# A chain of four modulated convolutions on one Trainium2 core: the prologue's instructions in another order

## The chip, the core and the metric

The kernel runs on one core of a Trainium2 chip. The core has a matrix engine (TensorE, PE in the profile, with its weight loads listed apart as PEld), VectorE (DVE), ScalarE (ACT) and GpSimd (POOL), each with an instruction list of its own that it works through in order, and DMA queues that are issued mainly by SyncE (SP). Engines wait for each other through semaphores. The metric is the device time of one execution in microseconds; the median of three runs before the change is 489.17 (488.39 to 489.69).

## The reference

The input `x` has 128 samples of 64 channels by 1024 positions. Each sample has a style vector of 128 numbers. Four layers are applied in a chain, and the input is added at the end. Each layer scales its 64x64x3 weight by input channel with a number from the style (modulation), and then by output channel so that the weight's sum of squares is one (demodulation):

```
s = style @ mw.T + mb
weight = SCALE * w * s[:, None, :, None]
demod = lax.rsqrt(jnp.sum(weight * weight, axis=(2, 3)) + EPS)
weight = weight * demod[:, :, None, None]
'same':       out = conv(x, weight) + b
'upsample':   out = blur(conv_transpose(x, weight, stride 2) + b, 2 * [1,3,3,1]/8, pad (1, 1))
'downsample': out = conv(blur(x, [1,3,3,1]/8, pad (2, 2)), weight, stride 2) + b
...
x + layers(x)          # same, upsample, same, downsample
```

Everything is linear in `x`, so away from the two ends the chain is one convolution with nine taps per sample, plus a constant per channel.

## The kernel before

The kernel builds that nine-tap weight for each sample and convolves once. Samples are worked on four at a time: a group `q` (32 of them) is two pairs, the two halves of the 128 partitions carrying different samples. The order of instructions is the order in which the program is written (a manual schedule): each engine's list is what the code issues to it, one after the other.

Building the weight of a group is a chain of three stages on TensorE, with a scaled copy out of PSUM behind each, done by ScalarE and, for group 0, by ScalarE and VectorE for one half each (`BOTH`):

- `scale3(q)`: `wd`, the last layer's weight scaled by the table `tA`, which needs layer 2's demodulation.
- `stage1(q)`: `psS`, the product of layer 2's and layer 3's weights, copied to `S` with the scale `tB`.
- `stage2(q)`: `psR`, `S` times the blurred upsampling taps `E`, copied to `R` with the scale `tC`, which needs the demodulation of layers 0 and 1.
- `stage3(q, part)`: `psW`, times layer 0's weight, copied to `Wf` with `t0`.

`E` doesn't depend on a sample: `blur_scale` makes four scaled copies `w1s` of layer 1's weight on ScalarE, `blur_matmul` adds them up on TensorE in `Y`, and `blur_copy` copies `Y` to `E`. In the profile of before its matmuls are L333, its copies L346 and L348.

The nine taps are applied as three interleaved planes of `x` with three taps each, by five products in place of nine. `combine_a` and `combine_b` form the weights `H` of products 1 to 3 on VectorE; `in_g01`, `in_g2`, `in1`, `in2`, `in3` and `in04` form their inputs `G` and `T` from the loaded `X`. `conv3`, `conv1`, `conv2`, `conv4` and `conv0` are the products, each of 12 matmuls with 340 columns (24 records, since a float32 matmul leaves two), L612. Between them `sum1` (the tile `y`, VectorE) and `sum2` read and combine the accumulators; `conv2` adds to the bank that `sum1` reads, so it waits for `sum1`.

The constants of the bias go through the layers in three small steps, `const_first(l)` on TensorE (L767) and `const_rest(l)` on VectorE (the tile `cc`, L783 and L784); `const_first(1)` needs what `const_rest(0)` writes, and stands in TensorE's list right behind `conv3(0)`.

The prologue works on the first 16 samples (`first`). `mod_matmul` (L193) makes the modulations `sc`; `mod_matmul(LATER, ...)` makes those of the other 112 samples, which a ScalarE copy takes to `raw` (L976). `var_matmul` (L220) or `first_var_matmul` (L233) make the sums of squares; `var_root` (L245, L246) and `newton` (L252 to L254) the demodulations `d` (layer 2) and `dm`. `q2_sum` adds the three taps' squared weights `wsq`. `zeros_to_y` clears the two banks of `Y` by matmuls with zeros. In the loop behind the prologue TensorE's list for one group holds its five products, `stage2` of the group after next and `stage3`, and `stage1` of the one behind that.

The prologue's order, up to the loop, is lines 946 to 1050 of the kernel. The functions that the change touches are these:

Of the kernel before, what the change touches and what calls it, by code (L numbers as in the profile page):

```python
# [63 lines left out]
def kernel(  # L64
# [121 lines left out]
    def by_layer(ps, bs):  # L186
        n = bs.stop - bs.start
        return ps[:, : NL * n].rearrange("c (l b) -> c l b", l=NL)

    def mod_matmul(bs, ps, ls=range(NL)):  # L190
        for l in ls:
            for cols in HALF:
                nc.tensor.matmul(  # L193
                    by_layer(ps, bs)[cols, l], mwT[:, l], styT[:, bs], start=True, stop=True
                )

    def mod_scale(bs, src, ls):
        m = mbs[:, ls, None].to_broadcast([P, ls.stop - ls.start, bs.stop - bs.start])
        nc_v.scalar_tensor_tensor(
            sc[:, ls, bs], by_layer(src, bs)[:, ls], SCALE, m, op0=ALU.mult, op1=ALU.add  # L200
        )
# [11 lines left out]
    def q2_sum(ls):  # L213
        nc_v.tensor_add(q2[T, ls], wsq[T, ls, 0, :], wsq[T, ls, 1, :])
        nc_v.tensor_add(q2[T, ls], q2[T, ls], wsq[T, ls, 2, :])

    def var_matmul(bs, ps, ls=range(NL), start=True):
        for l in ls:
            for cols in HALF:
                nc.tensor.matmul(  # L220
                    by_layer(ps, bs)[cols, l],
                    q2[T, l, :],
                    ssq[T, l, bs],
                    start=start,
                    stop=True,
                    skip_group_check=not start,
                )

    def first_var_matmul(bs, ps):

        for k in range(K):
            for cols in HALF:
                nc.tensor.matmul(  # L233
                    by_layer(ps, bs)[cols, 2],
                    wsq[T, 2, k, :],
                    ssq[T, 2, bs],
                    start=(k == 0),
                    stop=(k == K - 1),
                )

    def var_root(bs, src, ls=slice(0, NL), dst=None):

        src = by_layer(src, bs)[:, ls]
# [12 lines left out]
    def first_inverse(bs, src):  # L256

        var_root(bs, src, slice(2, 3), d2[:, None])
        newton(var[:, 2, bs], d2, n2)
# [52 lines left out]
    def blur_scale(ks):  # L312
        for i in ks:
            nc_a.activation(w1s[:, i], w1r, AF.Copy, scale=BLUR2[i])

    def blur_matmul(ps, ks):


        n = len(BLUR2)
        plan = [[], []]  # L320
        for b in range(n):
            for r, (lo, hi) in enumerate(((0, 5), (5, NT))):
                i, j = max(lo, b), min(hi, b + K)
                if i < j:
                    plan[r].append((b, i, j, lo))
        plan[1].reverse()
        for k in ks:
            for r, rows in enumerate(HALF):
                if k >= len(plan[r]):
                    continue  # L330
                b, i, j, lo = plan[r][k]
                for cols in HALF:
                    nc.tensor.matmul(  # L333
                        ps[r][cols, C * (i - lo) : C * (j - lo)],
                        idn[rows],
                        w1s[rows, min(b, n - 1 - b), i - b : j - b],
                        start=False,
                        stop=(k == len(plan[r]) - 1),
                        skip_group_check=True,
                    )  # L340

    def blur_copy(ps, engs):
        for r, (i, j) in enumerate(((0, 5), (5, NT))):
            dst, src = E[:, i:j].rearrange("c e i -> c (e i)"), ps[r][:, : (j - i) * C]
            if engs[r] is nc_a:
                nc_a.copy(dst, src)  # L346
            else:
                engs[r].tensor_copy(dst, src)  # L348
# [24 lines left out]
    def scale3(q, engs=(nc_a, nc_a)):  # L373
        wd = []
        src = w3 if q < DIRECT else w3x
        n = src.shape[1]
        for j in range(2):
            t = wd_pool.tile([P, 5, C], F32, tag="wd", name=f"wd{q}_{j}")
            scaled_copy(engs[j], t[:, :n], src, tA[:, q, j : j + 1])
            wd.append(t)  # L380
        chain[q] = wd
# [22 lines left out]
    def stage1(q, pool=None, engs=(nc_a, nc_a), between=None):  # L404

        wd = chain[q]
        ps = unit(pool or ps_w, f"psS{q}")
        for k, (at, at1) in enumerate(((0, 3), (3, 1), (1, 4))):
            tap_matmul(ps, wd, at, 2, woi[2][:, k, :], EVEN, first=k == 0)
            tap_matmul(ps, wd, at1, 1, woi[2][:, k, :], slice(1, 2), last=k == K - 1)  # L410
        if between:
            between()
        st, _ = s_tiles(q)
        for r in range(2):
            scaled_copy(engs[r], flat(st[r][:, 1:]), ps[r][:, : 5 * C], tB[:, q, r : r + 1])
        chain[q] = st
        return ps
# [24 lines left out]
        nc_g.tensor_add(t[:, :, 2], t[:, :, 2], t[:, :, 0])  # L442
        chain[q] = st

    def stage2(q, pool=None, engs=(nc_a, nc_a), among=(), between=None):
        st = chain[q]
        ps = unit(pool or ps_w, f"psR{q}")
        for n, e in enumerate((-2, -1, 0, 1, 2, 3, 4, 5, 6)):
            if n in among:
                among[n]()  # L450
            if e % 2 == 0:
                a, lo, m = slice(1, 4), e // 2 + 1, 3
            else:
                a, lo, m = slice(4, 6), (e + 3) // 2, 2
            for r, rows in enumerate(HALF):
                for c, cols in enumerate(HALF):
                    src = st[c if r == 0 else 1 - c]
                    nc.tensor.matmul(  # L458
                        ps[r][cols, lo * C : (lo + m) * C],
                        E[rows, e + 2, :],  # L460
                        src[rows, a, :],
                        start=(n == 0),
                        stop=(n == 8),
                        skip_group_check=True,
                    )
        if between:
            between()
        rt = []
        for r in range(2):
            t = r_pool.tile([P, 7, C], F32, tag="R", name=f"R{q}_{r}")  # L470
            scaled_copy(
                engs[r], t.rearrange("c t o -> c (t o)"), ps[r][:, : 7 * C], tC[:, q, r : r + 1]
            )
            rt.append(t)
        chain[q] = rt
        return ps
# [247 lines left out]
    def scaled_weights():  # L724
        for t, f in zip(w0s[1:], (1.0 / 3.0, -2.0)):
            nc_g.tensor_scalar_mul(t, woi[0], f)
        nc_g.tensor_scalar_mul(idn3, idn, 1.0 / 3.0)
# [232 lines left out]
    nc_v.tensor_scalar_mul(mbs, mb, SCALE)  # L960
    mod_matmul(first, pm[0][0], (2, 3))
    nc_a.activation(wsq[T, 2], wio[2][T], AF.Square)
    blur_scale(range(4))
    mod_matmul(first, pm[1][0], (0, 1))
    mod_scale(first, pm[0][0], slice(2, 4))
    mod_square(first, L2)
    first_var_matmul(first, pm[0][1])
    mod_scale(first, pm[1][0], L01)
    mod_square(first, L01)
    mod_square(first, L3)  # L970
    table_B(first)
    table_0(first)
    mod_matmul(LATER, pm[1][1])
    first_inverse(first, pm[0][1])
    nc_a.activation(wsq[T, 3], wio[3][T], AF.Square)
    nc_a.copy(raw[0][:, 0, :n_later], pm[1][1][:, :n_later])  # L976
    blur_matmul(psB, range(2))
    table_A(first, d2)
    scale3(0, BOTH)
    for l in range(2):  # L980
        nc_a.activation(wsq[T, l], wio[l][T], AF.Square)
    q2_sum(L3)
    scaled_weights()
    weight_sums(0)
    stage1(0, None, BOTH, lambda: blur_matmul(psB, range(2, 5)))
    blur_copy(psB, BOTH)
    q2_sum(L01)
    q2_sum(L2)
    scale3(1)
    scale3(2)  # L990

    def rest_of_var():
        var_matmul(first, pm[0][1], (0, 1, 3))

    def rest_of_scales():
        var_root(first, pm[0][1])
        var_newton(first)
        table_C(first, nc_v)

    stage2(0, None, BOTH, {4: rest_of_var}, rest_of_scales)  # L1000
    for of in (vector_c0, table_3, vector_a1, vector_Da, vector_b1, vector_c2):
        of(first)
    weight_sums(1, 2)
    stage1(1, ps_conv)
    in_g01(0, PAIR[0])
    in_g01(0, PAIR[1])
    stage3(0, 0, None, BOTH)
    in3(0)
# [1 line left out]
    const_first(0, first)  # L1010
    stage1(2)
    combine_a(0)
    in_g2(0)
    load(NX)
    split_weights()
    in1(0, nc_v)
    combine_b(0)
    const_rest(0, first, const_of(0, first))
    in2(0, nc_v)
    stage2(1, ps_conv)  # L1020
    conv3(0)
# [276 lines left out]
```

## Time and profile before

| what | us |
|---|---|
| median of three runs | 489.17 |
| lowest and highest run | 488.39, 489.69 |
| the profiled execution | 490.47 |
| its span, first to last instruction | 488.7 |
| TensorE busy in the span | 478.6 (98%) |
| VectorE busy | 383.4 (78%) |
| ScalarE busy | 289.6 (59%) |
| GpSimd busy | 143.2 (29%) |

The profiled execution is longer than the three timed runs, so a sum of its durations is compared with its own time first. A row of the view in order of time gives the start, the duration, the engine, the line, the operation with the tile that it writes and those that it reads, the shapes, the number of records merged, and in brackets how long the engine idled before it and what ended the idle time. A matmul's end is modelled, and successive ones overlap; where the text speaks of a pace, it goes from start to start.

### The profile page before, as it was taken

To read this page: it belongs to the slowest core of one execution; us is meant where nothing else is said; L and a number is where in the kernel's file an instruction comes from. 1 tells how busy PE (TensorE), PEld (TensorE's weight loads), DVE (VectorE), ACT (ScalarE), POOL (GpSimd) and SP (SyncE) were. 2 spreads that over 40 slices of the span, in tenths; PEclk is the share of its full clock that TensorE was granted. 3 is DMA by queue.
4 is the path that set the end of the run, shared out by engine and by line. 5 is a ranking of instruction groups with operands and counts; after the bars stand their busy time and mean duration, and the time that the engine had idled before them with its cause. 6 is when DMAs were issued, how large, how long until landed. Compare 5 with 4: busy or idle time off the path is not lost.

```text
span 488.7 us, 22181 instructions
## 1 busy us (share of the span) xinstructions
PE 478.6 (98%) x10048; PEld 383.5 (78%) x10048; DVE 383.4 (78%) x631; ACT 289.6 (59%) x578; POOL 143.2 (29%) x173
## 2 busy tenths in 40 slices
PE   8989999999999999999999999999999999999995
PEld 6967878777899877778888887878887877888863
DVE  3888887887888868976868988758988776988783
ACT  4546666567566657556566656656656666566542
POOL 2629125441335323113322123322123231212300
PEclk9989999999999999999999999999999999999999
DMA  7032544434334442344442344442344543245225
GB/s 247 19 130 71 202 165 175 175 125 141 116 147 175 175 172 81 116 164 170 175 148 78 128 172 175 175 147 67 141 172 175 175 174 117 95 159 175 90 87 173
DMA packets 20303, 70.42 MB, mean 144 GB/s; under 512 B 2288, under 2 KB 3824, under 8 KB 20208
## 3 DMA queue, kind: packets, MB, share of 16 engines
q1 hardware_dynamic: 19840, 68.53, 39.6%
q8 instruction: 79, 1.29, 1.0%
q10 hardware_dynamic: 368, 0.46, 0.3%
q14 instruction: 16, 0.13, 0.1%
HBM read 35.36 MB, written 33.62 MB: 141 GB/s over the span
## 4 chain that ended last, share of the span: by engine, by line
PE 95%; DVE 2%; DMA 1%; POOL 1%; issue 0%; ACT 0%; DVEq 0%
PE psA L612 45%; PE psR L458 16%; PE psW L499 15%; PE Y L612 11%; PE psS L386 5%; PE psE L843 2%; DMA par<-in_params 1%; DVE H L520 0%; PE Y L333 0%; PE psM L193 0%; POOL td L281 0%; DVE G L520 0%; DVE T L585 0%; DVE Wf L359 0%; DVE T L570 0%
## 5 line engine op out<-in xcount | busy, mean ns | idle before, releaser
L612 PE MATMUL psA<-T,H 64*64 64x340 f32 x2304 | 197.1, 449 | 0.2 <-DVE y L520 0.2
L612 PEld LDWEIGHTS psA<-T,H 64*64 64x64 f32 x2304 | 104.6, 134 | 44.0 <-issue 12.0
L442 POOL TENSOR_TENSOR S<-S 128x128 f32<-128x128 f32 x29 | 13.7, 471 | 290.5 <-ACT S L357 290.5
L458 PE MATMUL psR<-S,E 64*64 64x192 f32 (+1 forms) x2304 | 87.5, 299 | 0.5 <-ACT E L346 0.5
L458 PEld LDWEIGHTS psR<-S,E 64*64 64x64 f32 x2304 | 82.3, 133 | 5.7 <-ACT E L346 0.7
L357 ACT ACTIVATE R<-psR,tC 128x448 f32<-128x448 f32 x63 | 36.5, 630 | 68.8 <-PE psR L458 67.3
L612 PE MATMUL psA<-T,Wf 64*64 64x340 f32 x768 | 76.5, 447 | 0.0
L520 DVE SCALAR_TENSOR_TENSOR G<-X 128x1376 f32<-128x1376 f32 (+2 forms) x66 | 76.3, 1196 | 0.0
L357 ACT ACTIVATE Wf<-psW,t 128x384 f32<-128x384 f32 (+1 forms) x126 | 56.3, 497 | 14.6 <-PE psW L499 14.6
L499 PE MATMUL psW<-R,w0s 64*64 64x128 f32 (+1 forms) x1536 | 64.2, 289 | 0.0
L612 PE MATMUL Y<-T,Wf 64*64 64x340 f32 x768 | 62.2, 446 | 0.1
L499 PEld LDWEIGHTS psW<-R,w0s 64*64 64x64 f32 x1536 | 54.1, 133 | 5.9 <-ACT Wf L357 0.8
L520 DVE SCALAR_TENSOR_TENSOR Y<-m,psA 128x680 f32<-128x680 f32 (+1 forms) x33 | 28.0, 849 | 36.0 <-PE psA L612 35.5
L599 DVE TENSOR_TENSOR T<-G 128x1368 f32<-128x1368 f32 (+1 forms) x33 | 50.8, 1541 | 0.1
L681 ACT ACTIVATE o<-Y,tb,td 128x340 f32<-128x340 f32 x64 | 37.1, 630 | 22.3 <-ACT R L357 16.8
L520 DVE SCALAR_TENSOR_TENSOR y<-psA,m 128x680 f32<-128x680 f32 (+1 forms) x33 | 27.8, 844 | 28.7 <-PE psA L612 28.0
L585 POOL TENSOR_TENSOR T<-G 128x684 f32<-128x684 f32 x30 | 49.8, 1660 | 0.1
L590 POOL TENSOR_TENSOR T<-G 128x684 f32<-128x684 f32 x30 | 49.5, 1650 | 0.0
L386 PEld LDWEIGHTS psS<-wd,w2n 64*64 64x64 f32 x1160 | 41.3, 133 | 8.2
L612 PEld LDWEIGHTS Y<-T,Wf 64*64 64x64 f32 x768 | 36.1, 133 | 12.7 <-issue 0.6
L681 ACT ACTIVATE o<-psA,tb,td 128x340 f32<-128x340 f32 x63 | 36.6, 633 | 14.8 <-PE psA L612 14.8
L520 DVE SCALAR_TENSOR_TENSOR H<-Wf 128x384 f32<-128x384 f32 x64 | 40.5, 634 | 0.0
(148 smaller groups left out, 533.1 us busy)
## 6 DMA issues: line engine op xcount, KB each, us to landing
X<-in_x SPq DMA_DIRECT2D x64, 516.0 KB, 4.5
out<-o SPq DMA_DIRECT2D x60, 510.0 KB, 5.3
out<-o SPq DMA_DIRECT2D x6, 170.0 KB, 4.1
out<-o SPq DMA_DIRECT2D x2, 340.0 KB, 3.1
Xe<-in_x_ends SPq DMA_DIRECT2D x1, 512.0 KB, 6.4
par<-in_params SPq DMA_DIRECT2D x2, 192.0 KB, 3.6
out<-o ACTq DMA_DIRECT2D x2, 170.0 KB, 4.1
par_s<-in_params_s SPq DMA_DIRECT2D x1, 196.0 KB, 3.3
```

The lines of the kernel that those rows point to most:

```text
L357: nc_a.activation(dst, src, AF.Copy, scale=f)
L386: nc.tensor.matmul(ps[r][cols, at * C : (at + n) * C], weight[rows], wd[c if r == 0 else 1 - c][rows, taps], start=first, stop=last, skip_ ...
L442: nc_g.tensor_add(t[:, :, 2], t[:, :, 2], t[:, :, 0])
L458: nc.tensor.matmul(ps[r][cols, lo * C : (lo + m) * C], E[rows, e + 2, :], src[rows, a, :], start=(n == 0), stop=(n == 8), skip_group_check ...
L499: nc.tensor.matmul(ps[r][cols, at : at + m * C], w0s[kind][rows, k, :], rt[c][rows, first : first + K * (m - 1) + 1 : K, :], start=(n == 1 ...
L520: nc_v.scalar_tensor_tensor(out, x, f, y, op0=ALU.mult, op1=op)
L585: eng.tensor_add(t[:, :, 0, :NJ], plane(g, 2), plane(g, 1))
L590: eng.tensor_sub(t[:, :, 1, :NJ], plane(g, 2), plane(g, 1))
L599: nc_v.tensor_sub(t[:, pairs, :, :NJ], both(a, PL), both(b, 1))
L612: nc.tensor.matmul(ps[s][cols, :NB], w, Ts[q, tag][rows, c, i, g : g + NB], start=(g == 0 and m == 3), stop=(g == K - 1), skip_group_check ...
L681: nc_a.activation(dst, src, AF.Identity, bias=add, scale=d3)
L843: nc.tensor.matmul(ps[r][cols, : HB * n].rearrange("c (b j) -> c b j", j=n), weight(i, r, c)[rows], moving(i, r, c)[rows], start=(i == 0), ...
```

## The change

Only the prologue is written in another order; the loop and its functions stay. The matmuls of all blurred taps stand in one piece ahead of `stage1(0)`, and both halves of `E` are copied by ScalarE. Layer 2's sum of squares is first added up on VectorE (`q2_sum(L2)`) and then takes two matmuls; `first_var_matmul` goes. Four matmuls with zeros (128 columns) are added ahead of it. The modulations of the later samples are split into two pieces: layers 0 and 1 between `stage1(0)`'s matmuls and its copies, behind the variance of layers 0, 1 and 3, which stood inside `stage2(0)`; layers 2 and 3 behind `stage2(0)`, and their ScalarE copy there too. `in_g01(0, PAIR[0])`, the first half of the first `G`, moves from behind `stage1(1)` to right behind `stage1(0)`. GpSimd makes `a1` and `b1s` ahead of `t3`, and `const_rest(0)` moves from behind `combine_b(0)` to behind `combine_a(0)`.

```diff
-    def first_var_matmul(bs, ps):
-
-        for k in range(K):
-            for cols in HALF:
-                nc.tensor.matmul(
-                    by_layer(ps, bs)[cols, 2],
-                    wsq[T, 2, k, :],
-                    ssq[T, 2, bs],
...
-    def stage2(q, pool=None, engs=(nc_a, nc_a), among=(), between=None):
+    def stage2(q, pool=None, engs=(nc_a, nc_a), between=None):
...
     nc_a.activation(wsq[T, 2], wio[2][T], AF.Square)
-    blur_scale(range(4))
+    blur_scale(range(2))
     mod_matmul(first, pm[1][0], (0, 1))
+    zeros_to_y(2, 128, False)
     mod_scale(first, pm[0][0], slice(2, 4))
     mod_square(first, L2)
-    first_var_matmul(first, pm[0][1])
+    q2_sum(L2)
+    var_matmul(first, pm[0][1], (2,))
...
-    mod_matmul(LATER, pm[1][1])
     first_inverse(first, pm[0][1])
+    blur_scale(range(2, 4))
     nc_a.activation(wsq[T, 3], wio[3][T], AF.Square)
-    nc_a.copy(raw[0][:, 0, :n_later], pm[1][1][:, :n_later])
-    blur_matmul(psB, range(2))
+    blur_matmul(psB, range(5))
     table_A(first, d2)
     scale3(0, BOTH)
     for l in range(2):
         nc_a.activation(wsq[T, l], wio[l][T], AF.Square)
+    blur_copy(psB, (nc_a, nc_a))
     q2_sum(L3)
+    q2_sum(L01)
     scaled_weights()
     weight_sums(0)
-    stage1(0, None, BOTH, lambda: blur_matmul(psB, range(2, 5)))
-    blur_copy(psB, BOTH)
-    q2_sum(L01)
-    q2_sum(L2)
+
+    def rest_of_var():
+        var_matmul(first, pm[0][1], (0, 1, 3))
+        mod_matmul(LATER, pm[1][1], (0, 1))
+
+    stage1(0, None, BOTH, rest_of_var)
+    in_g01(0, PAIR[0])
     scale3(1)
     scale3(2)
-
-    def rest_of_var():
-        var_matmul(first, pm[0][1], (0, 1, 3))
...
-    stage2(0, None, BOTH, {4: rest_of_var}, rest_of_scales)
-    for of in (vector_c0, table_3, vector_a1, vector_Da, vector_b1, vector_c2):
+    stage2(0, None, BOTH, rest_of_scales)
+    mod_matmul(LATER, pm[1][1], (2, 3))
+    nc_a.copy(raw[0][:, 0, :n_later], pm[1][1][:, :n_later])
+    for of in (vector_c0, vector_a1, vector_b1, table_3, vector_Da, vector_c2):
         of(first)
     weight_sums(1, 2)
     stage1(1, ps_conv)
-    in_g01(0, PAIR[0])
     in_g01(0, PAIR[1])
...
     combine_a(0)
+    const_rest(0, first, const_of(0, first))
     in_g2(0)
     load(NX)
     split_weights()
     in1(0, nc_v)
     combine_b(0)
-    const_rest(0, first, const_of(0, first))
     in2(0, nc_v)
```

Line numbers of the changed kernel are 12 to 14 lower. On TensorE, from the modulations of the first samples (`psM_171`) to the first matmul of `stage1(0)` (`psS_0`), before:

```order
L193 MATMUL psM_171<-par_s 64x16 x4
L233 MATMUL psM_170<-ssq,wsq 64x16 x6
L193 MATMUL psM_171<-par_s 64x112 x8
L333 MATMUL Y<-w1s,par 64x192 x8
L386 MATMUL psS_0_248<-wd_0_235,par 64x128
```

and after:

```order
L193 MATMUL psM_171<-par_s 64x16 x4
L169 MATMUL Y<-Z 64x128 x4
L220 MATMUL psM_170<-ssq,q_129 64x16 x2
L321 MATMUL Y<-w1s,par 64x192 x10
L321 MATMUL Y<-w1s,par 64x128 x4
L321 MATMUL Y<-w1s,par 64x64 x4
L374 MATMUL psS_0_255<-wd_0_238,par 64x128
```

The eight matmuls of the later samples (112 columns) have left this stretch, and the ten blur matmuls that stood behind `stage1(0)` have come into it.

On ScalarE, from layer 2's demodulation (`d`) to the last `wd` of the prologue, before:

```order
L245 ACTIVATE d_131<-psM_170,eps 128x16
L975 ACTIVATE wsq<-par 64x192
L976 COPY raw_143<-psM_171 128x448
L357 ACTIVATE wd_0_235<-par,tA 128x192
L981 ACTIVATE wsq<-par 64x192 x2
L357 ACTIVATE S_284<-psS_0_248,tB 128x320
L346 COPY E<-Y 128x320
L357 ACTIVATE wd_0_293<-par,tA 128x192
```

and after:

```order
L233 ACTIVATE d_131<-psM_170,eps 128x16
L302 ACTIVATE w1s<-par 128x192 x2
L963 ACTIVATE wsq<-par 64x192
L345 ACTIVATE wd_0_238<-par,tA 128x192
L968 ACTIVATE wsq<-par 64x192 x2
L334 COPY E<-Y 128x320
L334 COPY E<-Y 128x256
L345 ACTIVATE S_291<-psS_0_255,tB 128x320
```

The copy to `raw` no longer stands between `wsq` and `wd`, and `E` is copied ahead of `S`, both halves here.

On VectorE, from the third `H` (which `conv3(0)` needs) on, before:

```order
L520 SCALAR_TENSOR_TENSOR H_403<-H_403,Wf_402 128x384
L520 SCALAR_TENSOR_TENSOR G_397<-X_105 128x2x342
L585 TENSOR_TENSOR T_0_489<-G_397 128x2x342
L520 SCALAR_TENSOR_TENSOR H_403<-Wf_402 128x384
L520 SCALAR_TENSOR_TENSOR H_403<-Wf_402,H_403 128x384
L520 SCALAR_TENSOR_TENSOR H_403<-H_403,Wf_402 128x384
L783 TENSOR_TENSOR cc_152<-Y,a_145 128x16
L784 SCALAR_TENSOR_TENSOR cc_152<-b1s,cc_152 128x16
```

and after:

```order
L506 SCALAR_TENSOR_TENSOR H_403<-H_403,Wf_402 128x384
L769 TENSOR_TENSOR cc_152<-Y,a_145 128x16
L770 SCALAR_TENSOR_TENSOR cc_152<-b1s,cc_152 128x16
L506 SCALAR_TENSOR_TENSOR G_294<-X_105 128x2x342
L571 TENSOR_TENSOR T_0_491<-G_294 128x2x342
L506 SCALAR_TENSOR_TENSOR H_403<-Wf_402 128x384
L506 SCALAR_TENSOR_TENSOR H_403<-Wf_402,H_403 128x384
L506 SCALAR_TENSOR_TENSOR H_403<-H_403,Wf_402 128x384
```

The two `cc` rows have moved ahead of five others; nothing else moved among these.

More of the change, by code (lines that the diff above doesn't have):

```diff
@@ L226, in var_matmul @@
                     skip_group_check=not start,
-                )
-    def first_var_matmul(bs, ps):
-        for k in range(K):
-            for cols in HALF:
-                nc.tensor.matmul(
-                    by_layer(ps, bs)[cols, 2],
-                    wsq[T, 2, k, :],
-                    ssq[T, 2, bs],
-                    start=(k == 0),
-                    stop=(k == K - 1),
                 )
@@ L448, in stage2 @@
         for n, e in enumerate((-2, -1, 0, 1, 2, 3, 4, 5, 6)):
-            if n in among:
-                among[n]()
             if e % 2 == 0:
```

## The prediction

> **What bounds the kernel now.** I read the page first, then the busy times in windows of 3.41 us, then TensorE, ScalarE and VectorE in order of time up to 35 us, since nothing behind that is edited.
>
> ```profile
> span 488.7 us, 22181 instructions
> PE 478.6 (98%) x10048; PEld 383.5 (78%) x10048; DVE 383.4 (78%) x631; ACT 289.6 (59%) x578; POOL 143.2 (29%) x173
> PEclk9989999999999999999999999999999999999999
> ```
>
> TensorE is busy 98% of the span and the loop behind the prologue leaves it no gap worth the name, so a microsecond counts if it brings forward the moment from which TensorE runs unbroken, and if it runs at full clock from there. The third tenth of the clock row is below 9: the clock dropped once, inside the prologue.
>
> ```profile
> 3.64:7.05 3.41, 2.75 (x38) 2.64 (x40) 1.49 (x9) 2.00 (x7) 1.04 (x5) 1.00 0.91 231
> 7.05:10.46 3.41, 3.41 (x62) 2.81 (x62) 1.64 (x7) 1.39 (x4) 2.29 (x5) 1.00 0.98 351
> ...
> 24.12:27.53 3.41, 1.53 (x47) 1.27 (x46) 3.24 (x8) 0.72 (x1) 0.00 (x0) 1.00 0.85 306
> 27.53:30.94 3.41, 3.41 (x38) 2.80 (x34) 2.97 (x6) 2.15 (x6) 0.00 (x0) 0.50 0.01 2
> 30.94:34.36 3.42, 3.23 (x60) 1.86 (x56) 2.58 (x5) 1.89 (x7) 1.20 (x3) 1.00 0.02 5
> ```
>
> The first numbers are the window and TensorE's busy time, the third from the end the granted clock. In 24.12:27.53 TensorE worked 1.53 us and idled 1.88; in the window right behind it, and in that one alone, the clock was 0.50. The first 10.5 us say 1.00, but the weight loads contradict it:
>
> ```profile
> L386 PEld LDWEIGHTS psS<-wd,par 64*64 64x64 f32 x36 | 1.6, 220 | 0.2
> ...
> L333 PEld LDWEIGHTS Y<-w1s,par 64*64 64x64 f32 x20 | 0.7, 134 | 0.0
> ```
>
> The first row is from 9 to 10.4 us, the second from 10.5 to 11.6: the same 64x64 load falls from 220 to 134 ns. So TensorE starts slow and goes to full speed at 10.46. A window with 2.75 us of work (3.64:7.05) did not lift the clock, a full one (7.05:10.46) did.
>
> **The prologue on TensorE.**
>
> ```profile
> 5.34 0.83 PE L233 MATMUL psM<-ssq,wsq 64*64 64x16 f32 x12 [0.17 <-ACT w1s L314]
> 6.09 1.76 PE L193 MATMUL psM<-par_s 128*64 128x112 f32 x16
> 7.79 1.56 PE L333 MATMUL Y<-w1s,par 64*64 64x192 f32 x16
> 9.12 1.82 PE L386 MATMUL psS<-wd,par 64*64 64x128 f32 x48
> 10.77 0.82 PE L333 MATMUL Y<-w1s,par 64*64 64x192 f32 x20
> 12.12 1.32 PE L458 MATMUL psR<-S,E 64*64 64x192 f32 x32 [0.53 <-ACT E L346]
> ...
> 15.02 1.22 PE L386 MATMUL psS<-wd,par 64*64 64x128 f32 x48
> 16.28 1.04 PE L499 MATMUL psW<-R,par 64*64 64x192 f32 x22
> ...
> 20.03 2.66 PE L458 MATMUL psR<-S,E 64*64 64x192 f32 x69
> ...
> 26.29 0.23 PE L767 MATMUL Y<-cc,wsum 64*64 64x16 f32 x2 [1.88 <-DVE cc L784]
> ...
> 28.23 3.33 PE L612 MATMUL psA<-T,H 64*64 64x340 f32 x24
> ...
> 31.44 0.99 PE L499 MATMUL psW<-R,w0s 64*64 64x128 f32 x22
> 32.61 1.95 PE L612 MATMUL psA<-T,H 64*64 64x340 f32 x24 [0.18 <-DVE y L520]
> ```
>
> Columns: start, duration, operation and, in brackets, the idle time before it and its releaser. The two gaps of size are at 12.12 (R waits for E) and 26.29. The last row is where TensorE's unbroken run begins; it waits for `y` on VectorE:
>
> ```profile
> 7.34 0.53 DVE L284 TENSOR_TENSOR tA<-sc,d 64x8 f32<-64x8 f32 x2
> ...
> 8.62 0.22 DVE L215 TENSOR_TENSOR q<-q,wsq 64x64 f32<-64x64 f32 x1
> ...
> 15.17 0.34 DVE L284 TENSOR_TENSOR tC<-dm 64x8 f32<-64x8 f32 x2
> 15.61 0.68 DVE L359 TENSOR_SCALAR R<-psR,tC 128x448 f32<-128x448 f32 x1
> 16.21 1.65 DVE L520 SCALAR_TENSOR_TENSOR G<-X 128x688 f32<-128x688 f32 x2
> 18.30 0.62 DVE L359 TENSOR_SCALAR Wf<-psW,t 128x384 f32<-128x384 f32 x1 [0.44 <-POOL b1s L737]
> ...
> 25.70 0.17 DVE L783 TENSOR_TENSOR cc<-Y,a 128x16 f32<-128x16 f32 x1
> ...
> 29.12 0.87 DVE L570 TENSOR_TENSOR T<-X 128x684 f32<-128x684 f32 x1 [0.34 <-issue]
> ...
> 31.69 0.87 DVE L520 SCALAR_TENSOR_TENSOR y<-psA,m 128x680 f32<-128x680 f32 x1
> ```
>
> From 18.30 to 32.57 VectorE has one listed pause, 0.34 us. Its list there is the same before and after, but for the order, so `y` moves by what the first Wf row moves, and no more than about 0.34 beyond that.
>
> **The change, part by part.** ScalarE's rows and the landing of the first X transfer:
>
> ```profile
> 7.90 0.53 ACT L976 COPY raw<-psM 128x448 f32<-128x448 f32 x1 [1.18 <-PE psM L193]
> 8.33 0.46 ACT L357 ACTIVATE wd<-par,tA 128x192 f32<-128x192 f32 x1
> 8.69 0.60 ACT L981 ACTIVATE wsq<-par 64x192 f32<-64x192 f32 x2
> 11.04 0.53 ACT L357 ACTIVATE S<-psS,tB 128x320 f32<-128x320 f32 x1 [1.76 <-PE psS L386]
> 11.64 0.43 ACT L346 COPY E<-Y 128x320 f32<-128x320 f32 x1
> 11.97 1.49 ACT L357 ACTIVATE wd<-par,tA 128x192 f32<-128x192 f32 x4
> 13.78 0.31 ACT L245 ACTIVATE dm<-psM,eps 128x64 f32<-128x64 f32 x1 [0.33 <-PE psM L220]
> ...
> X<-in_x SPq DMA_DIRECT2D x1, 516.0 KB, 6.2
> ```
>
> *Layer 2's variance.* Six matmuls (0.83) become two behind two VectorE adds (0.22 each and the step between). Four matmuls off at about 0.06 each against 0.5 of adds, part of it in TensorE's 0.17 pause: I take zero, bounds -0.1 and +0.3. Half of the w1s scalings move behind `d` on ScalarE, which idles there before the raw copy. The four added zero matmuls run while VectorE adds: zero. The adds push the second modulation, and with it GpSimd's tables tB and t0, back by half a microsecond; they are first read by the copies of S after 10 us, so that is hidden.
>
> *wd.* The raw copy leaves ScalarE's path: tA ends at 7.87, so wd starts there and not at 8.33.
>
> *Blur and S on TensorE.* The later samples' matmuls (1.70, from 6.09 to 7.79) leave. The blur starts near 6.1. Its first 16 records take 9.12 - 7.79 = 1.33; the other 20 took 0.6 start to start at full clock, and at the slow clock about 0.6 x 220 / 134 = 1.0, an estimate. So S starts at about 8.5 instead of 9.12, takes 10.77 - 9.12 = 1.65, and its copies start near 10.4 instead of 11.04.
>
> *E.* ScalarE is through with wsq at about 8.9, and two E copies of 0.43 end at 9.8, ahead of S: the 0.53 gap goes. S is copied by 10.95. Under it TensorE does six variance matmuls (0.3) and half of the later samples' (0.85 slow, 0.43 at full clock), until 10.9 to 11.4. R starts at 11.1, not 12.12: -1.0, bounds -0.6 and -1.2.
>
> *R, tC, S(1), W.* ScalarE's four wd (1.49) and dm (0.31) end at 12.8; VectorE in between does the first G (half of 1.65; X was issued at 4.3 and lands near 10.5, so it just makes it). From dm's end to tC's end it was 15.51 - 14.09 = 1.42, so tC is ready at 14.2 and R copied by 14.9 (16.29 before). TensorE: R about 2.4 (2.66 with its drain), the other half of the later samples 0.43, S(1) 16.28 - 15.02 = 1.26: W starts at 15.2. TensorE and not the copies decides, with 0.3 to spare. W: 15.2 against 16.28, -1.05. The raw copy then stands behind R on ScalarE (0.53), done by 15.5, before S(1) can be copied.
>
> *VectorE to `y`.* Wf at 17.25, `y` done at 31.5, and the convolution of 32.61 starts at 31.5: -1.1; with the 0.34 pause gone too, -1.45.
>
> *The constants' inputs.* cc (two rows, some 0.4 us) now stands ahead of G2; the same work, so `y` doesn't move. POOL's a1 and b1s, which it reads, go ahead of t3, which waits some 0.4 us longer and is first read at H's time, five microseconds later. No DMA changes its place in a queue; the next X load waits for G2 as before. TensorE no longer waits at 26.29: its third-product convolution ends at 24.41 - 1.05 = 23.36, W(1,0) takes 28.23 - 26.29 = 1.94, the next convolution 1.95 at full clock: done at 27.2. But then it has only the 0.99 us of 31.44 until `y` at 31.5. The idle time isn't gone; 1.88 in front becomes 3.3 behind, directly ahead of the unbroken run.
>
> *The clock.* In the windows of the row above, 27.53:30.94 then holds some 2.4 us of idleness (all but the 0.99 of work), more than the 1.88 that brought the clock to 0.50. So 30.94:34.36 runs at half clock, and there TensorE is the bound. The convolution of 24 takes 1.95 at full clock and 3.33 at half, so each slow microsecond loses 1 - 1.95 / 3.33 = 0.41, a window 1.4. Before, this price fell on the convolution of 28.23, whose end VectorE was hardly waiting for. If only half of the window lies behind 31.5, it is 0.7. If the clock stays low for a second window, as it did after 2.75 of 3.41 us of work at the start, it is 6.8 x 0.41 less what lies ahead of 31.5, some 2.4.
>
> The Trainium skill ("TensorE: Matmul & The Clock Gate", "What's actually happening" and "Why this matters for your kernels") lets the clock fall after an idle window of about 3.4 us, and warns of gaps over about 3 us. By that neither the 1.88 us nor the new gap would cost anything, and the sum would be -1.1. The trace disagrees at 1.88 us, so the sum goes by the trace. The same page calls the window free-running, so its place may differ from run to run; no run here shows that yet.
>
> **Sum.** -1.1 + 1.4 = +0.3. The profiled execution took 490.47 (span 488.7 and 1.8 around it), 1.3 above the median of 489.17 and above all three runs; on it 490.8, on the median 489.5.
>
> **Rivals.** *The clock stays full*, because the 1 us of work in the middle is enough or because the gap would have to be longer: -1.1, 488.1; with the pause gone 487.7. For it: only one drop is in the trace. Against: that drop came after less idleness. (The Trainium skill's limit of the page above would make it so.)
>
> *Two slow windows, slower than before:* -1.1 + 2.4, 490.5 to 490.8. For it: 2.75 of 3.41 us of work didn't lift the clock at the start. It decides from the point at which the slow window begins more than 3.41 - 2.75 = 0.7 us before `y` is done; in the windows of the rows above it would begin at 30.94, just short of that. Against: those 2.75 us were smaller matmuls than a convolution's.
>
> *The prologue gains little:* the later samples' matmuls in the gaps, 2 x 0.85 if TensorE is still slow there, and an X that lands late hold R and W; the gain shrinks from 1.1 to 0.4 (W waits 0.7 to 0.8 more), and with the slow window it is 490.2.
>
> **Chances.** One slow window 0.50 (489.0 to 490.2), clock full 0.20, two windows 0.20, little gain 0.10. 0.3% is 1.5 us, about what can be told from no change here; most of these cases lie within it. Faster by that, below 487.7: half of the second case and a little for gains not seen, 0.14. Slower, above 490.6: half of the third and the fourth, and a fifth of the first, whose prices add up to more if W is late as well, 0.26. Same 0.60. The range goes from 487.7 to 491.0.
>
> **What would show it.** R's first matmul near 11.1, W's near 15.2, the first Wf on VectorE near 17.25, `y` near 30.6; no wait before the cc matmul, a gap of over 2 us right before the convolution that follows `y`, and a clock of 0.5 for 3.4 us over it. The forecast is wrong if that convolution takes 1.95, if Wf comes later than 17.8, or if VectorE is not busy through from Wf to `y`.

## The result, and the profile after

The changed kernel takes 488.23 us (median of 22 runs, 486.93 to 489.87), the kernel before, run beside it on the same chip, 488.94 (22 runs, 487.94 to 489.69): a ratio of 0.9986 [0.9978, 0.9994], 0.7 us faster. The forecast was 489.5, 0.3 us slower. The number lies in the forecast's range; the direction was wrong.

The page of the changed kernel (profiled execution: 488.43 us):

```profile
span 486.6 us, 22180 instructions
PE 478.0 (98%) x10048; PEld 366.9 (75%) x10048; DVE 381.0 (78%) x630; ACT 289.9 (60%) x579; POOL 140.8 (29%) x173
```

Its TensorE rows in order of time:

```profile
7.89 2.13 PE L374 MATMUL psS<-wd,par 64*64 64x128 f32 x46
...
11.04 2.73 PE L444 MATMUL psR<-S,E 64*64 64x192 f32 x72
...
15.29 0.94 PE L485 MATMUL psW<-R,par 64*64 64x192 f32 x24
...
27.13 0.23 PE L753 MATMUL Y<-cc,wsum 64*64 64x16 f32 x2 [0.61 <-DVE cc L770]
...
30.18 2.99 PE L598 MATMUL psA<-T,H 64*64 64x340 f32 x24 [1.96 <-DVE y L506]
32.93 3.39 PE L444 MATMUL psR<-S,E 64*64 64x192 f32 x72
...
53.98 1.90 PE L598 MATMUL psA<-T,H 64*64 64x340 f32 x24
```

R starts at 11.04 without a wait and W at 15.29, both as forecast. The unbroken run begins at 30.18, behind a gap of 1.96 us that VectorE's `y` ends. Its first convolution takes 2.99 us. The windows of 3.41 us there (first numbers: the window and TensorE's work; third from the end: the granted clock):

```profile
24.12:27.53 3.41, 2.79 (x64) 1.63 (x57) 3.31 (x6) 2.16 (x6) 0.00 (x0) 1.00 0.55 222
27.53:30.94 3.41, 1.45 (x34) 0.84 (x29) 3.38 (x7) 2.68 (x8) 0.37 (x1) 1.00 0.03 7
30.94:34.36 3.42, 3.42 (x44) 2.09 (x40) 1.46 (x3) 0.06 (x1) 3.26 (x4) 0.50 0.58 181
```

The half clock has moved by one window, onto the start of the unbroken run, as forecast too. What was not forecast stands in VectorE's rows. After:

```profile
17.16 0.62 DVE L347 TENSOR_SCALAR Wf<-psW,t 128x384 f32<-128x384 f32 x1 [1.82 <-PE psW L485]
...
20.91 0.87 DVE L506 SCALAR_TENSOR_TENSOR G<-X 128x684 f32<-128x684 f32 x1
21.82 0.87 DVE L571 TENSOR_TENSOR T<-G 128x684 f32<-128x684 f32 x1
...
26.81 0.18 DVE L770 SCALAR_TENSOR_TENSOR cc<-c2f,cc 128x16 f32<-128x16 f32 x1
26.91 0.87 DVE L556 TENSOR_TENSOR T<-X 128x684 f32<-128x684 f32 x1
...
29.27 0.86 DVE L506 SCALAR_TENSOR_TENSOR y<-psA,m 128x680 f32<-128x680 f32 x1
```

From Wf to `y` it is 29.27 - 17.16 = 12.11 us, where the profile of before had 31.69 - 18.30 = 13.39. So VectorE needed 1.3 us less for the same rows.

### The profile page after: what moved, and what is told of

Read it like the earlier page. It is cut to its first block, busy times and chain, and to the rows that moved or that the text cites. A ratio compares the mean times of both kernels' runs of the same rounds, so it can differ in the third digit from the quotient of the medians.

```text
span 486.6 us, 22180 instructions
## 1 busy us (share of the span) xinstructions
PE 478.0 (98%) x10048; PEld 366.9 (75%) x10048; DVE 381.0 (78%) x630; ACT 289.9 (60%) x579; POOL 140.8 (29%) x173
## 4 chain that ended last, share of the span: by engine, by line
PE 96%; DVE 3%; issue 0%; DVEq 0%
PE psA L598 45%; PE psR L444 16%; PE psW L485 14%; PE Y L598 11%; PE psS L374 5%; PE psE L829 2%; PE Y L169 1%; PE Y L321 1%; DVE G L506 1%; DVE H L506 0%; PE psM L193 0%; DVE T L585 0%; DVE T L556 0%; DVE Wf L347 0%; DVE T L571 0%
## 5 line engine op out<-in xcount | busy, mean ns | idle before, releaser
L598 PE MATMUL psA<-T,H 64*64 64x340 f32 x2304 | 193.9, 448 | 2.1 <-DVE y L506 2.0
L598 PEld LDWEIGHTS psA<-T,H 64*64 64x64 f32 x2304 | 96.2, 133 | 51.9 <-issue 13.6
L444 PEld LDWEIGHTS psR<-S,E 64*64 64x64 f32 x2304 | 81.1, 134 | 7.4 <-issue 0.6
L598 PE MATMUL psA<-T,Wf 64*64 64x340 f32 x768 | 74.7, 447 | 0.0
L485 PE MATMUL psW<-R,w0s 64*64 64x128 f32 (+1 forms) x1536 | 61.8, 287 | 0.0
L485 PEld LDWEIGHTS psW<-R,w0s 64*64 64x64 f32 x1536 | 51.5, 133 | 6.7
L374 PEld LDWEIGHTS psS<-wd,w2n 64*64 64x64 f32 x1160 | 39.4, 133 | 10.0
L598 PEld LDWEIGHTS Y<-T,Wf 64*64 64x64 f32 x768 | 33.6, 133 | 14.8 <-issue 0.6
```

Of the source, the lines that this page charges most:

```text
L374: nc.tensor.matmul(ps[r][cols, at * C : (at + n) * C], weight[rows], wd[c if r == 0 else 1 - c][rows, taps], start=first, stop=last, skip_ ...
L444: nc.tensor.matmul(ps[r][cols, lo * C : (lo + m) * C], E[rows, e + 2, :], src[rows, a, :], start=(n == 0), stop=(n == 8), skip_group_check ...
L485: nc.tensor.matmul(ps[r][cols, at : at + m * C], w0s[kind][rows, k, :], rt[c][rows, first : first + K * (m - 1) + 1 : K, :], start=(n == 1 ...
L598: nc.tensor.matmul(ps[s][cols, :NB], w, Ts[q, tag][rows, c, i, g : g + NB], start=(g == 0 and m == 3), stop=(g == K - 1), skip_group_check ...
```

## The experiments

The profile of before is of an execution (490.47 us) that is longer than all its 22 runs above. So the unchanged kernel was profiled again (e0), and differences are taken to this new profile.

### The kernel before, unchanged (e0)

> The kernel before, profiled a second time, as a yardstick. If the place of the clock's windows and the landing of the parameters vary from execution to execution, this profile differs from the first one in both (first: parameters at 4.10, half clock from 27.53 to 30.94), while Wf to y on VectorE stays at 13.4 us (18.30 to 31.69). If they are fixed, all three agree. Time: same, ratio 1.000 within 0.001.

Measured: 489.19, ratio 0.9997 [0.9988, 1.0005]. VectorE, then two TensorE rows (the view of the second ends at 56 us) and two windows:

```profile
18.06 0.62 DVE L359 TENSOR_SCALAR Wf<-psW,t 128x384 f32<-128x384 f32 x1 [0.45 <-POOL b1s L737]
...
21.71 1.13 DVE L520 SCALAR_TENSOR_TENSOR G<-X 128x684 f32<-128x684 f32 x1
22.87 1.01 DVE L585 TENSOR_TENSOR T<-G 128x684 f32<-128x684 f32 x1
...
28.36 0.18 DVE L784 SCALAR_TENSOR_TENSOR cc<-c2f,cc 128x16 f32<-128x16 f32 x1
28.88 0.87 DVE L570 TENSOR_TENSOR T<-X 128x684 f32<-128x684 f32 x1 [0.34 <-issue]
...
31.24 0.86 DVE L520 SCALAR_TENSOR_TENSOR y<-psA,m 128x680 f32<-128x680 f32 x1
```

```profile
32.15 1.95 PE L612 MATMUL psA<-T,H 64*64 64x340 f32 x24 [1.66 <-DVE y L520]
...
54.84 1.59 PE L612 MATMUL psA<-T,H 64*64 64x340 f32 x17
```

```profile
24.14:27.56 3.42, 1.54 (x52) 1.54 (x54) 3.25 (x7) 0.72 (x1) 0.00 (x0) 1.00 0.77 302
27.56:30.97 3.41, 2.94 (x64) 2.13 (x56) 2.97 (x6) 2.59 (x8) 0.00 (x0) 1.00 0.03 7
```

This gives the balance. Wf comes 0.90 earlier after the change (18.06 to 17.16), the stretch from Wf to `y` is 1.07 shorter (13.18 to 12.11), so `y` and the convolution behind it come 1.97 earlier (32.15 to 30.18). At the later convolution of 54.84 only 0.86 of it is left (53.98): the half clock took the other 1.1. Both parts are tested below. The clock also shows something: the same window, with 1.53 and 1.54 us of work, was followed by half clock in the first profile and not in this one.

### Where VectorE's time came from: GpSimd beside it

Rows that are longer before than after (G 1.13 against 0.87, T 1.01 against 0.87) have the same shapes. In e0 GpSimd works beside them; the first and last of its eight rows that make `wsum`, `w3x` and `w2n`, in e0 and then in the changed kernel:

```profile
18.18 0.31 POOL L717 TENSOR_TENSOR wsum<-par 128x64 f32<-128x64 f32 x1
...
22.07 1.08 POOL L369 TENSOR_TENSOR w2n<-par 128x128 f32<-128x128 f32 x1
```

```profile
15.86 0.32 POOL L703 TENSOR_TENSOR wsum<-par 128x64 f32<-128x64 f32 x1
...
18.85 0.45 POOL L357 TENSOR_TENSOR w2n<-par 128x128 f32<-128x128 f32 x1
```

GpSimd starts 1.6 us earlier after the change, since `dm` does, and meets less of VectorE's work, so that it takes 6.0 us (13.3 to 19.3) instead of 8.2 (15.0 to 23.2) for the whole list. Theory: its work lengthens VectorE's rows, and the change gains by taking part of it away from beside them. Rival: the rows are shorter for another reason of the new order. The test moves GpSimd's work alone, in the kernel before (e3):

```diff
     weight_sums(0)
+    weight_sums(1, 2)
+    split_weights()
...
-    weight_sums(1, 2)
     stage1(1, ps_conv)
...
     load(NX)
-    split_weights()
```

> The kernel before with GpSimd's sums and copies of weights (weight sums of layers 1 and 2, w3x, w2n; some 4 us) in its idle time from 10 to 15 us, instead of 18.4 to 23.4 beside VectorE. Contention theory (VectorE's rows in the chain from Wf to y are longer while GpSimd works): Wf to y 0.5 to 0.7 us shorter than 13.4, and the total 0.5 us less, ratio 0.999. Rival (VectorE's chain got shorter in the changed kernel only because the pauses at cc went away): chain as before, ratio 1.000.

Measured: 488.79, ratio 0.9990 [0.9980, 0.9999]. GpSimd makes these tiles at 9.7 to 13.0, and on VectorE:

```profile
18.02 0.62 DVE L359 TENSOR_SCALAR Wf<-psW,t 128x384 f32<-128x384 f32 x1 [0.38 <-PE psW L499]
...
21.24 0.86 DVE L520 SCALAR_TENSOR_TENSOR G<-X 128x684 f32<-128x684 f32 x1
22.14 0.87 DVE L585 TENSOR_TENSOR T<-G 128x684 f32<-128x684 f32 x1
...
28.01 0.87 DVE L570 TENSOR_TENSOR T<-X 128x684 f32<-128x684 f32 x1 [0.35 <-issue]
...
30.37 0.86 DVE L520 SCALAR_TENSOR_TENSOR y<-psA,m 128x680 f32<-128x680 f32 x1
```

Wf hardly moves, and from Wf to `y` it is 12.35 instead of 13.18: 0.83 us, from an order on GpSimd alone. The lengthening is shown to be GpSimd's. The Trainium skill ("SBUF — State Buffer", "Who interferes with whom") says that a VectorE instruction with two SBUF inputs contends with a GpSimd instruction that reads SBUF, since its second input comes through a read interface that the two share. G, T and H have two such inputs and the trace agrees, with 16% on T and 30% on G.

The same move in the changed kernel (e9):

```diff
     weight_sums(0)
+    weight_sums(1, 2)
+    split_weights()
...
-    weight_sums(1, 2)
     stage1(1, ps_conv)
...
     load(NX)
-    split_weights()
```

> The changed kernel with GpSimd's weight sums and copies in its idle time before 13 us, and nothing else. y comes 0.2 to 0.3 us earlier; the gap ahead of the convolution stays, and with it the slow window in most executions (mean clock 0.994): ratio 0.998 by the contention theory, and 0.9986 if it is worth nothing here.

Measured: 488.23, ratio 0.9984 [0.9975, 0.9992]. Wf to `y` is 11.86, another 0.25 less: of the 0.83 us that GpSimd cost the kernel before, the change had taken away about 0.6. But `y` then comes at 28.93, the gap ahead of the convolution is 2.05 us, and half clock follows it. The total can't be told from the changed kernel's.

The pause of 0.34 us between the second cc and T is left. It is in every profile in which GpSimd makes `t3` ahead of `a1` and `b1s` (before, e0, e2, e3) and in none with the other order. Only that line was changed in e10:

```diff
-    for of in (vector_c0, table_3, vector_a1, vector_Da, vector_b1, vector_c2):
+    for of in (vector_c0, vector_a1, vector_b1, table_3, vector_Da, vector_c2):
```

> The kernel before with one line of the change: GpSimd makes a1 and b1s ahead of t3. If that order is what takes the pause of 0.34 us behind the second constant's step away (it is there in all profiles with the old order and in none with the new one), the second cc and the T behind it follow at 0.1 us, Wf to y is 12.8 us instead of 13.2, ratio 0.999. Rival (the pause went with the place of the first constant's step): pause as before, ratio 1.000.

Measured: 488.79, ratio 0.9997 [0.9988, 1.0006]. On VectorE:

```profile
27.80 0.17 DVE L784 SCALAR_TENSOR_TENSOR cc<-c2f,cc 128x16 f32<-128x16 f32 x1
27.90 0.87 DVE L570 TENSOR_TENSOR T<-X 128x684 f32<-128x684 f32 x1
```

The pause is gone, and T starts 0.10 behind the cc instead of 0.52, so it was worth 0.42. From Wf to `y` it is 12.45, 0.73 less than in e0 where 0.4 was expected; most of the rest is shorter rows beside GpSimd, whose work also shifted (the first T behind Wf takes 0.95 instead of 1.02). The convolution behind `y` starts at 31.18 instead of 32.15, and still the total doesn't show it. How much of this chain reaches the total is thus not well known.

Why an order on GpSimd ten microseconds earlier brings the pause to VectorE stays open. It does change VectorE's own list. In e0 the second cc row of the first constant waits for GpSimd's `b1s` and has a semaphore instruction of its own ahead of it; in e10 it has neither, and starts 0.20 behind the first instead of 0.28. The traces have 795 records of VectorE, semaphore instructions included, in the four profiles with the pause and 793 or 794 in the ten without, so the T behind it has another place in the list. Whether that is the cause was not tested.

### The clock

Theory: the half clock follows from the idle gap of 1.96 us ahead of the convolution, and costs what the forecast said, since TensorE is the bound there. Rival: half clock there has another cause or is paid for anyway, and the earlier `const_rest(0)` gains by the gap that it takes away in front. First, work in the gap (e4): twelve matmuls with zeros, which add nothing to `Y`, behind the last cc matmul.

```diff
     const_first(2, PART[0])
+    for _ in range(3):
+        zeros_to_y(2, NB, False)
     sum1(0)
```

> The changed kernel with the same twelve matmuls with zeros, now directly behind the third constant's matmul (27.1 us in the changed kernel's profile), where nothing on VectorE has to read the tile first; W(1,1) follows them. Clock theory: TensorE idles less than 1 us ahead of the convolution behind y, no slow window falls on it, and every execution takes what the changed kernel's undisturbed ones took, 487.4 us (mean clock 0.997 and up), ratio to before 0.997. Rival (the gap has nothing to do with the low clock): mean clock 0.994 in two thirds of the executions as in the changed kernel, ratio 0.9986.

Measured: 488.31, ratio 0.9978 [0.9970, 0.9987]. TensorE:

```profile
27.41 1.94 PE L169 MATMUL Y<-Z 64*64 64x340 f32 x22
...
30.35 1.95 PE L598 MATMUL psA<-T,H 64*64 64x340 f32 x24 [0.25 <-DVE y L506]
```

The gap is filled and the convolution takes 1.95 us instead of 2.99. The total is 0.9 above the 487.4 that was expected. The kernel before took 489.43 beside it and 488.94 beside the change, which accounts for some 0.5; the rest is open. Next, the move of `const_rest(0)` undone in the changed kernel (e5), which puts part of the gap back in front:

```diff
-    const_rest(0, first, const_of(0, first))
...
     combine_b(0)
+    const_rest(0, first, const_of(0, first))
```

> The changed kernel with one part undone: the first constant's VectorE step stands behind combine_b again. Clock theory: TensorE's gap of 1.9 us lies in front again, ahead of W(1,0), the slow window, where it comes, falls on matmuls that VectorE is slower than anyway, y and the total keep the prologue's gain: 487.5 us in all executions, ratio 0.997, faster than the changed kernel although this wait is back. Rival (moving the constant's step is what gains): back to before, ratio 1.000.

Measured: 488.38, ratio 0.9980 [0.9972, 0.9989], with two gaps of 1.21 and 1.24 us:

```profile
30.41 1.95 PE L598 MATMUL psA<-T,H 64*64 64x340 f32 x24 [1.24 <-DVE y L506]
...
53.11 1.94 PE L598 MATMUL psA<-T,H 64*64 64x340 f32 x24
```

The convolution starts 0.23 us later than in the changed kernel, runs at full clock, and at 53 us TensorE is 0.87 ahead of it (53.11 against 53.98). Over the whole, e5 is no slower than the changed kernel, though 0.9 above the expected 487.5 as e4 is: the earlier `const_rest(0)` gained nothing. That move alone, with the new GpSimd order, in the kernel before (e6):

```diff
-    for of in (vector_c0, table_3, vector_a1, vector_Da, vector_b1, vector_c2):
+    for of in (vector_c0, vector_a1, vector_b1, table_3, vector_Da, vector_c2):
...
     combine_a(0)
+    const_rest(0, first, const_of(0, first))
...
     combine_b(0)
-    const_rest(0, first, const_of(0, first))
```

> That part alone, in the kernel before: the first constant's VectorE step behind combine_a, and a1 and b1s ahead of t3 on GpSimd. Clock theory: VectorE still sets y, at most 0.3 us sooner; the gap moves to the place ahead of the convolution behind y and grows to about 3 us, so slow windows cost 1.2 us in most executions: ratio 1.001 to 1.002. Rival (that wait was worth its 1.88 us): faster, ratio 0.997.

Measured: 489.98, ratio 1.0004 [0.9990, 1.0019]. No gain, though VectorE's chain from Wf to `y` is down to 12.25 us. TensorE, and the window ahead of its convolution with the one behind:

```profile
31.72 3.62 PE L612 MATMUL psA<-T,H 64*64 64x340 f32 x24 [1.96 <-DVE y L520]
```

```profile
28.34:31.75 3.41, 1.12 (x32) 0.81 (x32) 3.41 (x6) 1.96 (x8) 0.00 (x0) 1.00 0.07 23
31.75:35.16 3.41, 3.41 (x24) 1.52 (x28) 1.01 (x2) 0.79 (x2) 2.89 (x4) 0.50 0.37 88
```

The place of such a window differs between executions: of the fourteen profiles the clock first reaches 1 between 7.5 and 11.3 us, at 10.46 in both the first two. If windows of 3.41 us are laid on from that moment to 37 us in each profile, the four with at most 1.45 us of work (1.45 in the changed kernel, 1.36 in e9 and in e1 below, 1.12 in e6) were all followed by half clock, of the two with 1.54 one was, and of all others, from 1.69 up, none. So it is the work in a window of fixed place that decides, and a gap counts when most of it falls into one. The Trainium skill ("TensorE: Matmul & The Clock Gate", "What's actually happening") calls the window free-running, which the trace bears out, and asks for an idle window, which it doesn't: 1.45 us of work in 3.41 was too little.

How often it happens shows in the mean granted clock of each execution, which one such window lowers by 3.41 x 0.5 / 488 = 0.0035 (e0 has 0.997 without one, from elsewhere in its span). With less than 0.9965 counted as a drop: 15 of 22 executions of the changed kernel (488.60 us on average, the other 7 487.39), 8 of 12 of e6 (490.29 and 488.21), 7 of 12 of e9 (488.55 and 487.82), 8 of 12 of e1 below (491.39 and 489.30), none of 11 of e4, none of 11 of e5 and 1 of 9 of e7 below. Leaving e1 aside, where the added work is slowed too, the price is 0.7 to 2.1 us on average when it happens. Part of it may be a second window. The lowest mean clock of a profile without a drop is 0.997, so one window leaves about 0.9935, but four executions of e6 (490.86 on average; its other four with a drop 489.72) and the slowest of the changed kernel (489.87) have 0.991 or 0.992. None of these was profiled. By the changed kernel's executions it is 1.2 x 15 / 22 = 0.8 on the mean; by the ratios of e4 and e5 against the change's it is 0.3 to 0.4, with intervals that overlap. In the kernel before it costs nothing that shows: of its 96 executions beside the experiments, 11 with a drop average 489.38 and 85 without one 489.32.

Two fills went another way than meant. One stood directly ahead of `conv2(0)` in the changed kernel (e1):

```diff
     scale3(3)
+    for _ in range(3):
+        zeros_to_y(2, NB, False)
     conv2(0)
```

> The changed kernel with twelve matmuls with zeros (340 columns, 24 records) ahead of the convolution that waits for y, which fill the gap of 1.96 us. They change nothing in the result. Clock theory (the gap brings half clock onto TensorE's unbroken run, which costs 1.4 to 1.7 us in most executions): granted clock full but for the end, 1.0 to 1.4 us faster than the changed kernel, ratio to before 0.996. Rival (the gained time is lost elsewhere, to an engine that binds in the loop): same as the changed kernel, ratio 0.9986. If zeros don't count as work for the clock: slow window as before, ratio 0.9986 or a little worse.

Measured: 490.81, ratio 1.0025 [1.0011, 1.0039]. TensorE:

```profile
30.61 3.46 PE L169 MATMUL Y<-Z 64*64 64x340 f32 x24 [2.04 <-DVE oc L765]
33.84 2.13 PE L598 MATMUL psA<-T,H 64*64 64x340 f32 x24
```

The fill writes `Y`, which VectorE's `oc` was still to read, and so waited until behind `y`. The gap stayed, the fill itself ran at half clock, and its time was added. This says nothing for or against the theory's cause, but shows what unneeded work at half clock costs on the path. In the kernel before (e2), the fill stood behind `copy_m3(0)`, in the gap in front:

```diff
     copy_m3(0)
+    for _ in range(3):
+        zeros_to_y(2, NB, False)
     const_first(1, PART[0])
```

> The kernel before with the same twelve matmuls with zeros in its gap of 1.88 us, ahead of the constant's matmul that waits for cc. Clock theory: no slow window from 27.5 on, but there VectorE is what TensorE waits for, so TensorE only waits longer for y; time the same within 0.1%, with the gap of 1 to 1.5 us now right ahead of the convolution behind y. Rival (the slow window cost time in the kernel before too): faster by 1 us, ratio 0.998.

Measured: 489.60, ratio 1.0004 [0.9995, 1.0013].

```profile
26.03 1.95 PE L169 MATMUL Y<-Z 64*64 64x340 f32 x24 [1.51 <-DVE cc L783]
...
32.50 1.95 PE L612 MATMUL psA<-T,H 64*64 64x340 f32 x24 [0.31 <-DVE y L520]
```

The fill waited for cc and pushed the cc matmul from 26.05 (e0) to 27.80; the gap of 1.66 ahead of the convolution of `y` took that up, and the time is the same. So TensorE's list before `y` had 1.4 us of slack, and bringing the cc matmul forward could gain nothing.

### Versions that use the gap

Two changes together: `const_rest(0)` back behind `combine_b(0)` as in e5, and GpSimd's work ahead as in e3 (e8).

```diff
     weight_sums(0)
+    weight_sums(1, 2)
+    split_weights()
...
-    weight_sums(1, 2)
...
-    const_rest(0, first, const_of(0, first))
...
-    split_weights()
...
     combine_b(0)
+    const_rest(0, first, const_of(0, first))
```

> The changed kernel with the first constant's VectorE step behind combine_b again, and GpSimd's weight sums and copies in its idle time before 13 us. Contention theory: the T and H rows right behind Wf lose what GpSimd still adds to them there (1.17 to 0.87 and the like), Wf to y 11.8 us instead of 12.2, 0.3 us less than without the GpSimd part: ratio 0.9975. Clock theory: mean clock 0.997 and up in all executions. Rival (GpSimd's part is worth something in the kernel before only): ratio 0.998 as without it.

Measured: 487.93, ratio 0.9975 [0.9965, 0.9986], none of 7 executions with a drop. Useful work in the gap: the changed kernel with 16 of the 36 matmuls of `stage2(2)` ahead of `conv2(0)` (e7).

```diff
     def stage2(q, pool=None, engs=(nc_a, nc_a), between=None, among={}):
...
         for n, e in enumerate((-2, -1, 0, 1, 2, 3, 4, 5, 6)):
+            if n in among:
+                among[n]()
...
     scale3(3)
-    conv2(0)
...
-            stage2(c)
+            stage2(c, among={4: lambda: conv2(0)} if q == 0 else {})
```

> The changed kernel with the first 16 of the 36 matmuls of stage2(2) ahead of the convolution that waits for y instead of behind it: useful work in the gap. Clock theory: 1.1 us of work less behind y, no slow window: 486.3 us, ratio 0.994 to 0.995. Rival (VectorE or ScalarE binds right behind): the convolution starts at the same time, and later rows win nothing, ratio 0.997 at best.

Measured: 488.13, ratio 0.9973 [0.9964, 0.9982]. The work did move into the gap and the convolution ran at full clock, but less came of it than expected. A new wait further on, of TensorE for ScalarE, and what ScalarE waits for there:

```profile
39.82 1.29 PE L487 MATMUL psW<-R,w0s 64*64 64x128 f32 x22 [1.02 <-ACT Wf L345]
```

```profile
38.14 1.16 ACT L669 ACTIVATE o<-Y,tb,td 128x340 f32<-128x340 f32 x2 [2.26 <-DVE var L234]
```

TensorE is so early that ScalarE's Wf copies, which stand behind an `o` that waits for VectorE, aren't ready: 1.02 us are lost. With e8 as the base and half as many matmuls ahead (e11):

```diff
-            stage2(c)
+            stage2(c, among={2: lambda: conv2(0)} if q == 0 else {})
```

> The first kernel of these four with the first 8 of stage2(2)'s 36 matmuls ahead of the convolution that waits for y: 0.5 us of useful work in a gap of 1.2. Expected 0.3 to 0.5 us faster than without them, ratio 0.9965 to 0.997, unless VectorE's step for the second part's variance, late already with 16 of them, makes TensorE wait at W(2,1) again: then ratio 0.9975.

Measured: 487.97, ratio 0.9976 [0.9966, 0.9985], with 0.50 us of the same wait. So e7, e8 and e11 are 1.3 us faster than the kernel before and can't be told apart; against the changed kernel their intervals overlap. In e7 and e11 this wait points to VectorE behind `y`, by way of ScalarE, as the next limit in place of TensorE's gap.

## Why the prediction was wrong

- *E*, *Blur and S*, and *R, tC, S(1), W*: right in size. R at 11.04 (11.1), W at 15.29 (15.2), Wf at 17.16 (17.25). That it fits to 0.1 us is partly luck. TensorE's first modulation matmuls (L193), which need the parameters that a DMA brings, began at 3.56 in the changed kernel's profile and at 4.12 in the profile of before, so 0.56 of the time gained there isn't the change's. S was sized wrongly: it began at 7.7 instead of 8.5, but took 2.1 us at the slow clock rather than 1.65. Counted from those modulation matmuls it began 0.87 earlier than before, where 0.6 was forecast; the forecast took 0.06 for each of the four variance matmuls that fall away, but six of them take 6.09 - 5.34 = 0.75, so it is 0.125 each, 0.26 more in all. Over all profiles Wf comes at 18.20 on average with the old prologue (6) and at 17.27 with the new (8): -0.92 where -1.05 was forecast.
- *VectorE to `y`*: this step failed. It said that `y` moves by what the first Wf row moves and at most 0.34 more, because VectorE's list was the same. The list was, but not the durations of its rows: GpSimd's earlier work took some 0.6 us of lengthening away (0.83 in e3, less the 0.25 that e9 finds still there), and the new order of `a1` and `b1s` took the pause of 0.42 and a semaphore instruction of 0.08 away (e10). The stretch got 1.07 us shorter, and `y` came at 29.27 instead of about 30.6. The 1.02 us of T and the 1.12 of G in the profile of before, against 0.87 for rows of the same shape later, were there to be read. None of the three signs that the forecast named for being wrong appeared (the convolution took 2.99, Wf came at 17.16, VectorE was busy through); it shows in the time of `y`.
- *The constants' inputs*: right that it moves the gap behind. The gap was 1.96 us plus 0.61 ahead of the cc matmul, not 3.3, since `y` came earlier. That the cc matmul's wait was no loss is shown by e2.
- *The clock*: the mechanism was right: 0.50 from 30.94 to 34.36, on the path. That it was the very window of the forecast is luck, since the clock first rose at 10.46 in both profiles; and in 7 of 22 executions there was no such window. As a term it was mis-sized. The forecast took 1.4 us in every execution; it is 1.2 in 15 of 22. In the profiled execution the convolution and R took 1.68 us more than their 1.77 and 2.5 from start to start at full clock, and 0.6 of that came back by 53 us, as e5 shows (0.87 left of 1.46 at the row behind R).
- The sum: -0.9 for Wf, -1.1 for the chain, and +0.8 for the clock make -1.2, against -0.7 measured (0.4 to either side by its interval). Some 0.5 us of the gain is missing, and without the half clock too: the 7 executions without a drop lie 1.55 below the median of the kernel before, not the 1.97 of the convolution's start. Whether waits further on take it, as in e7, or single profiles stand for the average only that well, was not settled: from the start of the later convolution (53.98 and 54.84 above) to the end of the span it is 432.7 us in the changed kernel's profile and 432.8 in e0, but 432.6 to 434.1 over the fourteen.
- The rivals: the time of *the clock stays full* (488.1) came out almost exactly, but not its cause: the clock fell, and a gain that the sum lacked paid for it. *Two slow windows* is in none of the fourteen profiles, but the mean clock points to it in one execution of the changed kernel and four of e6.

## What to carry to other kernels

A list of instructions that stays the same doesn't take the same time: when an edit moves GpSimd's work, compare VectorE's rows of one shape with and without GpSimd beside them, and price the difference. Before closing a gap ahead of a waiting engine, look at where its idle time goes next: before `y` it was free, and directly ahead of the unbroken run it cost the clock. Where the price hangs on a window of the clock whose place varies, take it over many executions; one profile shows only one of two cases.

## What the runs showed of the hardware

- Half clock followed a window of 3.41 us with up to 1.45 us of TensorE work, in four profiles of four; with 1.54 in one of two, with 1.69 and more in none.
- The place of these windows differs from run to run (the first rise of the clock lies between 7.5 and 11.3 us), and with it whether a gap costs anything.
- GpSimd and VectorE slow each other: G 0.87 to 1.13, T 0.87 to 1.01 us on VectorE, and on GpSimd the last `w2n` 0.45 to 1.08.
- A pause of 0.34 us on VectorE came and went with the order of small GpSimd instructions, ten microseconds earlier. With that order VectorE's list changes by a semaphore instruction; no cause was shown.
